# A four-layer gated model on one core: the first cross-attention's keys and values move behind layer 0's first experts, with one unused product, and two row transfers go out a chunk from the eighth chunk

## The chip, the cores and the metric

The kernel runs on one core of one Trainium2 chip. The metric is the device time of one execution, in microseconds (us); several runs are made and their median is compared. The core has five engines with a queue each: TensorE (PE in the profile, with its weight loads as PEld), VectorE (DVE), ScalarE (ACT), GpSimd (POOL) and SyncE (SP, which here only issues transfers). Each works through its own queue in order, and semaphores tie the queues together. All data is float32 but for a mask.

## What is computed

The state X has 16 sequences of 128 tokens with 128 features. It passes four layers. Each layer adds to X a cross-attention with a context C of the same shape, times tanh of a gate, and then a feed-forward part, times tanh of another gate. Cut to what matters here:

```
layer 0: X += g * (Q + tril(C C^T) Q),  Q = norm(X)              # linear attention
         X += g * sum over the best 2 of 8 experts of  c_e * down_e(silu(gate_e x) * up_e x),  x = norm(X)
layer 1: q = norm(X) hW qW,  k = C cW kW,  v = C cW vW           # with biases
         X += g * (softmax(q k^T / sqrt(128)) v + q) oW
         X += g * (best 4 of 16 experts + 2 shared ones)
layers 2 and 3: 16-head attentions, a slot layer, and 32 experts
```

## The kernel before, in words

The 16 sequences are worked in four groups of four (GB = 4), so one tile has 128 features by 512 tokens. Layer 0's experts are done in two ways. Group 0 takes all eight experts densely: 16 chunks of 128 hidden features, each with two products of 128x512 (gate `pg` and up `pu`, in `gated`, L447), an activation on ACT (`sg`), a product `h` on DVE (L464), a product `hw` with the routing weight `cb` (L471 on DVE, L473 on POOL), and a down product into `acc` (L1128), two chunks later. Groups 1 to 3 are routed: their rows are scattered by expert into a table `xd` in HBM by 24 indirect transfers of POOL (`places_0`, L974, tile `xs`), and then worked in blocks of 128 rows that belong to one expert each (`blocks_0`: load `xb` from `xd` on SP's queue at L1040, transposes at L1047, products at L1069, silu at L1076, down product at L1024).

`experts` (L1120) is a generator that writes the whole order of the feed-forward work. While it goes through group 0's chunks n = 0 to 15, it takes steps of other generators in between. `SEND` (L890) says how many of the 24 scatters follow each chunk: 2, 1, 2, 1, 2 for chunks 5 to 9 and 2 for each of 10 to 15, which is 20. Two more follow the last chunk, and the last two are issued only after group 0's next normalisation (`sent_behind` is set to "rs"). A scatter may not pass the latest `hw` product of POOL (`behind_of("hw", ...)`, L112). `on_vector` (L895) says which share of `hw` DVE takes: none for chunks 0 to 4, three quarters for 5 to 9 (POOL takes the last quarter), all from 10. After chunk 9 `joined_1` multiplies the weights of layer 1's attention together in place. After chunk 12 the first half of `attention_1(0)` is taken: keys `kT` (one 128x512 product with L108, copied by ACT with a bias at L288) and values `v` (four 128x128 products, added to a bias by DVE at L591).

When the 16 chunks are done, `acc` is copied to `yT` on ACT (L1131), turned by four transposes (`end`, L1138) and added to X on DVE (L278). Then the second half of `attention_1(0)` runs: statistics on DVE (L251, L255, `ve` at L257), the inverse root `rs` on POOL (L259), the normalised rows `xn` on DVE (L270), four transposes (L241) with a copy to `xnTm` (L243), queries `qT` (L108, L288), scores (L108, `mm<-a,qT`), and the softmax (L313 to L380). The first half of `attention_1(1)` follows in the program, and then the blocks.

Each engine's queue is not the program's order word for word: a list scheduler orders the instructions when the program is built, by their place in the program and by what is ready. `in_turn(chain, ins)` (L439) pins an instruction behind the one before it in a chain, on the order alone. PSUM has four banks for "m" work (attention) and three for "x" work (experts).

Of the kernel before, what the change touches and what calls it, by code (L numbers as in the profile page):

```python
# [10 lines left out]
F32 = mybir.dt.float32  # L11
BF16 = mybir.dt.bfloat16
I32 = mybir.dt.int32
AF = mybir.ActivationFunctionType
ALU = mybir.AluOpType
AX = mybir.AxisListType

P = 128
B = 16
GB = 4  # L20
NG = B // GB
GT = GB * P
D = 128
CH = 512
EPS = 1e-5
# [34 lines left out]
def flamingo(ctx, tc, x_in, ctx_in, mask_in, w1, w2, w3, wslot, wsmall, slots, cols_in, rows_in, consts_in,  # L60
             gu0, dn0, gu1, dn1, gu3, dn3, out):
    nc = tc.nc
# [3 lines left out]
    act = ctx.enter_context(tc.tile_pool(name="act", bufs=2))  # L66
# [21 lines left out]
    def mm_tile():  # L88
        return bank("mm")
# [10 lines left out]
    def bc(ap, axis, n):  # L100

        a = ap.unsqueeze(axis)
        shape = list(a.shape)
        shape[axis] = n
        return a.to_broadcast(shape)

    def mm(o, l, r, start=True, stop=True):
        nc.tensor.matmul(out=o, lhsT=l, rhs=r, start=start, stop=stop)  # L108

    latest = {}  # L110

    def behind_of(what, ins):  # L112

        if what in latest:
            in_turn([latest[what]], ins)
# [65 lines left out]
    ident = const.tile([P, P], F32, tag="ident", name="ident")  # L181
# [32 lines left out]
    for i in range(0, NBLK * D, GB * VB):  # L214
        n = min(GB * VB, NBLK * D - i)
# [3 lines left out]
    def row(name):  # L219
        at, n = ROW[name]  # L220
        return rows[:, at:at + n]

    def col(name):
        i = COLS.index(name)
        return cols[:, i:i + 1]
# [7 lines left out]
    tgf = const.tile([P, 4], F32, tag="tgf", name="tgf")  # L233
    nc.scalar.activation(tgf[:], gates[:, 4:8], AF.Tanh)


    def transposed(src, tag, pool, bufs):

        pt = tr_tile()
        for t in range(GB):  # L240
            nc.tensor.transpose(pt[:, t * P:(t + 1) * P], src[:, t, :], ident[:])  # L241
        o = pool.tile([P, GT], F32, tag=tag, name=tag, bufs=bufs)
        nc.any.tensor_copy(o[:], pt[:])  # L243
        return o

    def normed(g, xn=None, on_act=False, behind=None):
        x = X[g]
        st = small.tile([P, GB, 6], F32, tag=tag_of("st"), name="st")
        mv = small.tile([P, GB, 2], F32, tag=tag_of("mv"), name="mv")
        for t in range(GB):  # L250
            ins = nc.vector.bn_stats(st[:, t, :], x[:, t, :])  # L251
            if t == 0 and behind is not None:
                behind_of(behind, ins)
        for t in range(GB):
            nc.vector.bn_aggr(mv[:, t, :], st[:, t, :])  # L255
        ve = small.tile([P, GB], F32, tag=tag_of("ve"), name="ve")
        nc.vector.tensor_scalar(ve[:], mv[:, :, 1], EPS, None, ALU.add)  # L257
        rs = small.tile([P, GB], F32, tag=tag_of("rs"), name="rs")
        latest["rs"] = nc.gpsimd.tensor_tensor(rs[:], ve[:], neghalf[:], ALU.pow).ins  # L259
        if xn is None:  # L260
            xn = act.tile([P, GB, D], F32, tag=tag_of("xn"), name="xn", bufs=1)
        if on_act:
            off = small.tile([P, GB], F32, tag="off", name="off")
            nc.gpsimd.tensor_tensor(off[:], mv[:, :, 0], rs[:], ALU.mult)
            latest["off"] = nc.gpsimd.tensor_scalar(off[:], off[:], -1.0, None, ALU.mult).ins
        for t in range(GB):
            if on_act:
                nc.scalar.activation(xn[:, t, :], x[:, t, :], AF.Identity, bias=off[:, t:t + 1], scale=rs[:, t:t + 1])
            else:
                nc.vector.tensor_scalar(xn[:, t, :], x[:, t, :], mv[:, t, 0:1], rs[:, t:t + 1], ALU.subtract, ALU.mult)  # L270
        return xn

    def normed_T(g):
        xn = normed(g)
        return xn, transposed(xn, tag_of("xnT"), act, 2 if side[0] == "x" else 1)
# [7 lines left out]
    def linear_T(w, src, tag, bias, bufs=None):  # L283

        p = mm_tile()
        mm(p[:], w, src[:])
        o = act.tile([P, GT], F32, tag=tag, name=tag, bufs=bufs)
        nc.scalar.activation(o[:], p[:], AF.Identity, bias=bias)  # L288
        return o
# [149 lines left out]
    def in_turn(chain, ins):  # L439

        if chain:
            tc.add_manual_dep(ins.ins, chain[-1].name,
                              mybir.DependencyInfo(mybir.DependencyClass.NoSync, mybir.DependencyReason.DATA),
                              reason="in_turn")
        chain[:] = [ins.ins]
# [65 lines left out]
    CT = []  # L511
# [47 lines left out]
    w = lambda W, i: W[:, i * D:(i + 1) * D]  # L559
# [23 lines left out]

    def attention_1(g):

        kT = linear_T(w(W1, 1), CT[g], "a0", bias=col("kb"))
        pv = split(mm_tile())
        for t in range(GB):
            mm(pv[:, t, :], CT[g][:, t * P:(t + 1) * P], w(W1, 2))
        v = act.tile([P, GB, D], F32, tag="a3", name="v1")  # L590
        nc.vector.tensor_tensor(v[:], pv, bc(row("vb"), 1, GB), ALU.add)  # L591
        yield
        _, xnT = normed_T(g)
        (nc.gpsimd if g else nc.vector).tensor_tensor(X[g][:], X[g][:], bc(ob1[:], 1, GB), ALU.add)
        qT = linear_T(w(W1, 0), xnT, "qT", bias=col("qb"))
        ps = split(mm_tile())
        for t in range(GB):
            b = slice(t * P, (t + 1) * P)
            mm(ps[:, t, :], qT[:, b], kT[:, b])
        e = softmax_exp(ps, GB, float(np.float32(1.0) / np.sqrt(np.float32(D))))  # L600
        pn = over_sum(e, P, "sm2", work)
        pts = transpose_probs(pn, P, P)
        po = acc_tile()
        for t in range(GB):
            mm(po[:, t * P:(t + 1) * P], v[:, t, :], pts[:, t, :])
        aT = act.tile([P, GT], F32, tag="oT", name="aT")
        nc.vector.tensor_tensor(aT[:], po[:], qT[:], ALU.add)
        py = split(mm_tile())
        for t in range(GB):
            mm(py[:, t, :], aT[:, t * P:(t + 1) * P], w(W1, 5))  # L610
        add_gated(g, py, tgx[:, 1:2])
        yield
# [274 lines left out]
    routed = {}  # L887


    SEND = [(n, 2 if n > 9 else 1 + n % 2) for n in range(5, 16)]  # L890
    FETCH = {0: [(n, 2) for n in range(4)] + [(n, 1) for n in range(4, 18)], 1: [(n, 1) for n in range(6)]}

    JOIN = 9

    def on_vector(layer, g, n):  # L895

        if (layer, g) == (0, BYE - 1):
            return 1 if n > 9 else 0.75 if n > 4 else 0
        return 1 if (layer, g) == (1, 0) and n < 4 else 0

    def with_tanh(layer, g):
# [218 lines left out]
    def experts():  # L1120


        chain, behind, ends = [], [], []
# [10 lines left out]
        def end():  # L1134
            layer, g, yT = ends.pop()
            pt = split(tr_tile())
            for t in range(GB):
                nc.tensor.transpose(pt[:, t, :], yT[:, t * P:(t + 1) * P], ident[:])  # L1138
            add_gated(g, pt, SHAPE[layer][2])
            if layer == 3:  # L1140
                nc.sync.dma_start(out[g * GB:(g + 1) * GB].rearrange("b s d -> s b d"), X[g][:])
            return layer, g

        for at, (layer, g) in enumerate(ORDER):
# [6 lines left out]
            ne, width, _ = SHAPE[layer]  # L1151
            xnT, cbs = routed.pop((layer, g))
            steps = {}
            moving = (layer, g) == (0, BYE - 1)
            if moving:
                for n, k in SEND:
                    steps.setdefault(n, []).extend([("m", sending, None)] * k)
                steps.setdefault(13, []).append(("m", "owners", None))
                steps.setdefault(JOIN, []).append(("m", joining, None))
                steps.setdefault(JOIN + 3, []).append(("m", context_1, None))  # L1160
            elif at + 1 < len(ORDER):
                nxt = routing(*ORDER[at + 1])
                for n in (12, 14, 15, 17) if (layer, g) == (1, 0) else (3, 7, 8, 13):
                    steps.setdefault(n, []).append(("x", nxt, None))
# [31 lines left out]
                        yield what  # L1196
            if moving:
                side[0] = "m"
                for _ in range(2):
                    next(sending)  # L1200
                side[0] = "x"
                while behind:
                    down()
                what = end()
                side[0] = "m"
                yield what
                sent_behind[0] = "rs"
                for _ in sending:
                    pass
                nxt = routing(1, 0)  # L1210
                for n, _ in enumerate(blocks_0()):
                    if n in (8, 11, 12, 15):
                        side[0] = "x"
                        next(nxt)
                    side[0] = "m"
# [28 lines left out]
    W1 = load("w1", w1)  # L1244
# [9 lines left out]
    sending, fetching = places_0(), return_0()  # L1254
# [10 lines left out]
    context_1 = attention_1(0)  # L1265
# [33 lines left out]
    for s in range(2):  # L1299
        for n in range(2):  # L1300
            nc.vector.tensor_copy(hcols[:, s, 3 * n:3 * n + 1], pp[:, 4 * s + 2 * n:4 * s + 2 * n + 1])
            hcol[f"bq{2 + n}{s}"] = hcols[:, s, 3 * n:3 * n + 1]
            for j in range(2):
                o = hcols[:, s, 3 * n + 1 + j:3 * n + 2 + j]
# [156 lines left out]
```

## Time and profile before

| | |
|---|---|
| median of 3 runs | 897.54 us (896.16 to 898.15) |
| the profiled execution | 894.61 us |
| its span, from first to last instruction | 892.9 us |
| mean granted TensorE clock | 0.979 |
| busy: PE, DVE, POOL, ACT | 92%, 64%, 33%, 30% of the span |
| PE of the chain that ended last | 54% |

The profiled execution is one run with its own time; durations and positions in the text come from it, with the span's start as zero. "Granted clock" is the share of the full TensorE clock that the chip gave: 1.00 or 0.50 nearly everywhere in this trace. A row of the timeline has start, duration, engine, line, operation, what it writes and reads, and in brackets how long the engine stood idle before it and what ended that. A row "x2" or "x8" has several records merged: a float32 product shows as two.

### The profile page before, as it was taken

To read this page: it belongs to the slowest core of one execution; us is meant where nothing else is said; L and a number is where in the kernel's file an instruction comes from. 1 tells how busy PE (TensorE), PEld (TensorE's weight loads), DVE (VectorE), ACT (ScalarE), POOL (GpSimd) and SP (SyncE) were. 2 spreads that over 40 slices of the span, in tenths; PEclk is the share of its full clock that TensorE was granted. 3 is DMA by queue.
4 is the path that set the end of the run, shared out by engine and by line. 5 is a ranking of instruction groups with operands and counts; after the bars stand their busy time and mean duration, and the time that the engine had idled before them with its cause. 6 is when DMAs were issued, how large, how long until landed. Compare 5 with 4: busy or idle time off the path is not lost.

```text
span 892.9 us, 16081 instructions
## 1 busy us (share of the span) xinstructions
PE 825.1 (92%) x6189; PEld 465.7 (52%) x6189; DVE 570.0 (64%) x1599; ACT 263.5 (30%) x473; POOL 296.0 (33%) x304
## 2 busy tenths in 40 slices
PE   6899799988998999998999989999999999999997
PEld 4554599444444544554555554555555544554443
DVE  5775434557878567468667666768766678667522
ACT  1522355232331221332232222232222232222321
POOL 3547321666452123014221114321033122313453
PEclk9999699999999999999999999999999999999999
DMA  9451122840311011002121114110002111111230
GB/s 280 160 124 52 48 83 70 246 127 15 107 60 36 33 41 36 25 25 65 44 61 45 50 37 131 50 37 24 25 25 75 49 37 52 69 49 61 86 113 29
DMA packets 55677, 62.12 MB, mean 70 GB/s; under 512 B 14312, under 2 KB 33512, under 8 KB 55472
## 3 DMA queue, kind: packets, MB, share of 16 engines
q1 hardware_dynamic: 53536, 57.67, 21.1%
q0 software_dynamic: 1536, 3.15, 1.2%
q8 instruction: 49, 0.80, 0.4%
q10 hardware_dynamic: 528, 0.26, 0.1%
q14 instruction: 28, 0.23, 0.1%
HBM read 53.97 MB, written 7.09 MB: 68 GB/s over the span
## 4 chain that ended last, share of the span: by engine, by line
PE 54%; DVE 20%; POOL 10%; issue 9%; ACT 3%; DMA 3%; POOLq 0%; SPq 0%; DVEq 0%; ACTq 0%
PE mm L108 8%; PE pu L453 7%; PE acc L1128 7%; PE pg L452 7%; POOL hw L473 6%; DVE sg L458 3%; PE po L499 3%; DVE mp L493 3%; PE mm L647 3%; DVE h L464 2%; POOL rs L259 2%; PE po L502 2%; PE pg L1069 2%; PE tr L241 2%; DVE xn L270 2%
## 5 line engine op out<-in xcount | busy, mean ns | idle before, releaser
L473 POOL TENSOR_TENSOR hw<-h,cb 128x512 f32<-128x512 f32 (+1 forms) x136 | 171.3, 1260 | 439.5 <-DVE h L464 352.9
L453 PE MATMUL pu<-xnTx,wall 128*128 128x512 f32 x288 | 153.1, 614 | 5.9 <-DVE sg L458 3.7
L452 PE MATMUL pg<-xnTx,wall 128*128 128x512 f32 x288 | 152.8, 613 | 1.1 <-ACT xnTx L243 0.7
L1128 PE MATMUL acc<-hw,wall 128*128 128x512 f32 x288 | 150.1, 605 | 0.5 <-POOL hw L473 0.5
L464 DVE TENSOR_TENSOR h<-sg,pu 128x512 f32<-128x512 f32 x147 | 100.4, 683 | 69.2 <-PE pu L453 57.7
L457 ACT ACTIVATE sg<-pg 128x512 f32<-128x512 f32 x105 | 62.8, 598 | 222.0 <-PE pg L452 213.4
L458 DVE SCALAR_TENSOR_TENSOR sg<-sg,pg 128x512 f32<-128x512 f32 x105 | 71.3, 679 | 32.9 <-ACT sg L457 32.8
L453 PEld LDWEIGHTS pu<-xnTx,wall 128*128 128x128 f32 x288 | 51.7, 192 | 65.7 <-issue 42.3
L1128 PEld LDWEIGHTS acc<-hw,wall 128*128 128x128 f32 x288 | 53.2, 194 | 56.0 <-issue 48.6
L493 DVE TENSOR_REDUCE mp<-mm 128x4 f32<-128x512 f32 (+1 forms) x112 | 65.7, 644 | 21.1 <-PE mm L647 19.9
L452 PEld LDWEIGHTS pg<-xnTx,wall 128*128 128x128 f32 x288 | 49.5, 192 | 40.5 <-issue 29.5
L507 DVE RECIPROCAL rcw<-po 128x128 f32<-128x128 f32 (+1 forms) x28 | 25.2, 900 | 52.8 <-PE po L502 41.9
L460 ACT ACTIVATE sg<-pg 128x512 f32<-128x512 f32 x51 | 30.4, 596 | 81.9 <-PE pg L452 81.8
L259 POOL TENSOR_TENSOR rs<-ve,neghalf 128x4 f32<-128x4 f32 x32 | 32.8, 1026 | 61.4 <-DVE ve L257 60.0
L499 PE MATMUL po<-pts,vp 128*32 128x128 f32 (+1 forms) x896 | 45.8, 273 | 6.4 <-ACT pts L669 5.5
L270 DVE TENSOR_SCALAR xn<-x,mv,rs 128x128 f32<-128x128 f32 x104 | 36.7, 408 | 21.5 <-POOL rs L259 21.5
L669 ACT ACTIVATE pts<-mm 128x512 f32<-128x512 f32 x64 | 33.8, 600 | 54.8 <-PE mm L663 54.3
L502 PE MATMUL po<-pts,own 128*32 128x128 f32 (+1 forms) x896 | 43.9, 265 | 0.0
L499 PEld LDWEIGHTS po<-pts,vp 128*32 128x32 f32 (+1 forms) x896 | 21.5, 108 | 29.4 <-ACT pts L669 14.3
L251 DVE BATCH_NORM_STATS2 st<-x 128x6 f32<-128x128 f32 x128 | 30.8, 301 | 8.9 <-DMA x<-in_x 8.3
L241 PE MATMUL tr<-ident,xn 128*128 128x128 f32 x100 | 23.3, 316 | 12.7 <-DVE xn L270 11.5
L647 PE MATMUL mm<-kTm,qT 32*128 32x256 f32 x256 | 30.5, 413 | 0.0
(354 smaller groups left out, 1234.4 us busy)
## 6 DMA issues: line engine op xcount, KB each, us to landing
cb<-combD SPq DMA_DIRECT2D x72, 256.0 KB, 3.4
cb<-combD SPq DMA_DIRECT2D x128, 128.0 KB, 2.9
wall<-in_gu SPq DMA_DIRECT2D x24, 256.0 KB, 5.0
wall<-in_dn SPq DMA_DIRECT2D x12, 256.0 KB, 4.8
xb<-xd SPq DMA_DIRECT2D x7, 256.0 KB, 2.8
yd<-yb SPq DMA_DIRECT2D x7, 256.0 KB, 2.3
xd<-vp SPq DMA_DIRECT2D x1, 1072.0 KB, 7.5
x<-in_x SPq DMA_DIRECT2D x4, 256.0 KB, 6.5
```

What stands on the lines that cost most here:

```text
L108: nc.tensor.matmul(out=o, lhsT=l, rhs=r, start=start, stop=stop)
L452: in_turn(chain, nc.tensor.matmul(out=pg[:], lhsT=w[:, 0], rhs=xnT[:], start=True, stop=True))
L453: in_turn(chain, nc.tensor.matmul(out=pu[:], lhsT=w[:, 1], rhs=xnT[:], start=True, stop=True))
L457: nc.scalar.activation(sg[:], pg[:], AF.Tanh, scale=0.5)
L458: nc.vector.scalar_tensor_tensor(sg[:], sg[:], 1.0, pg[:], ALU.add, ALU.mult)
L464: ins = nc.vector.tensor_tensor(h[:], sg[:], pu[:], ALU.mult)
L473: latest["hw"] = nc.gpsimd.tensor_tensor(hw[:, at:], h[:, at:], cb[:, at:], ALU.mult).ins
L493: nc.vector.tensor_reduce(mp[:, 0:n, 32 * i + 16:32 * i + 18], src, AX.X, ALU.max)
L499: in_turn(chain, nc.tensor.matmul(out=po[32 * jj:32 * jj + 32, 0, :], lhsT=vcols, rhs=pts, start=first, stop=last, skip_group_check=True))
L502: in_turn(chain, nc.tensor.matmul(out=po[32 * jj:32 * jj + 32, 1, :], lhsT=own[rows, r, :], rhs=pts, start=False, stop=last, skip_group_ch ...
L647: nc.tensor.matmul(out=split(ps[i])[:, 2 * s:2 * s + 2, :], lhsT=qT[rr, s, b], rhs=kTm[rr, s, :, b], start=False, stop=True, skip_group_ch ...
L1128: in_turn(chain, nc.tensor.matmul(out=acc[0][:], lhsT=w[:, 2], rhs=h[:], start=n == 0, stop=last))
```

## The change

Four edits:

1. The first half of `attention_1(0)` is no longer taken after chunk 12. The generator now runs through in one go, when group 0's experts are done. For group 0 the products are pinned on PE in this order: the four transposes of `yT`, keys, values, an unused product, the four transposes of `xn`. The normalisation stands ahead of the keys in the program, and DVE's addition for `v` is pinned behind `ve`.
2. `busy_with(512)` is the unused product: the identity by four copies of itself, into a bank of PSUM that nobody reads.
3. `SEND` gives two scatters to chunk 8 as well, so 21 fall to the chunks, one follows the last chunk instead of two, and the last two stay behind the normalisation.
4. `on_vector` gives all of `hw` to DVE from chunk 8 instead of chunk 10.

For the other groups `attention_1` does what it did.

```diff
+    def busy_with(n, chain=None):
+        o = mm_tile()[:, :n].rearrange("p (t d) -> p t d", d=P)
+        ins = nc.tensor.matmul(out=o, lhsT=ident[:], rhs=bc(ident[:], 1, n // P), start=True, stop=True)
+        if chain is not None:
+            in_turn(chain, ins)
...
-        nc.vector.tensor_scalar(ve[:], mv[:, :, 1], EPS, None, ALU.add)
+        latest["ve"] = nc.vector.tensor_scalar(ve[:], mv[:, :, 1], EPS, None, ALU.add).ins
...
     def attention_1(g):
-        kT = linear_T(w(W1, 1), CT[g], "a0", bias=col("kb"))
+        chain = [latest["yT"]] if g == 0 else None
+        if g == 0:
+            xn = normed(g)
+        p = mm_tile()
+        mm(p[:], w(W1, 1), CT[g][:], chain=chain)
+        kT = act.tile([P, GT], F32, tag="a0", name="a0")
+        nc.scalar.activation(kT[:], p[:], AF.Identity, bias=col("kb"))
         pv = split(mm_tile())
         for t in range(GB):
-            mm(pv[:, t, :], CT[g][:, t * P:(t + 1) * P], w(W1, 2))
+            mm(pv[:, t, :], CT[g][:, t * P:(t + 1) * P], w(W1, 2), chain=chain)
         v = act.tile([P, GB, D], F32, tag="a3", name="v1")
-        nc.vector.tensor_tensor(v[:], pv, bc(row("vb"), 1, GB), ALU.add)
-        yield
-        _, xnT = normed_T(g)
+        ins = nc.vector.tensor_tensor(v[:], pv, bc(row("vb"), 1, GB), ALU.add)
+        if g == 0:
+            behind_of("ve", ins)
+            busy_with(CH, chain)
+            xnT = transposed(xn, "xnTm", act, 1, chain)
+        else:
+            yield
+            _, xnT = normed_T(g)
...
-    SEND = [(n, 2 if n > 9 else 1 + n % 2) for n in range(5, 16)]
+    SEND = [(n, 2 if n > 7 else 1 + n % 2) for n in range(5, 16)]
...
         if (layer, g) == (0, BYE - 1):
-            return 1 if n > 9 else 0.75 if n > 4 else 0
+            return 1 if n > 7 else 0.75 if n > 4 else 0
...
-                nc.tensor.transpose(pt[:, t, :], yT[:, t * P:(t + 1) * P], ident[:])
+                latest["yT"] = nc.tensor.transpose(pt[:, t, :], yT[:, t * P:(t + 1) * P], ident[:]).ins
...
-                steps.setdefault(JOIN + 3, []).append(("m", context_1, None))
...
             if moving:
                 side[0] = "m"
-                for _ in range(2):
-                    next(sending)
+                next(sending)
```

More of the change, by code (lines that the diff above doesn't have):

```diff
@@ L105, in bc, with mm @@
         return a.to_broadcast(shape)
-    def mm(o, l, r, start=True, stop=True):
-        nc.tensor.matmul(out=o, lhsT=l, rhs=r, start=start, stop=stop)
+    def mm(o, l, r, start=True, stop=True, chain=None):
+        ins = nc.tensor.matmul(out=o, lhsT=l, rhs=r, start=start, stop=stop)
+        if chain is not None:
+            in_turn(chain, ins)
     latest = {}
@@ L234, in flamingo, with transposed @@
     nc.scalar.activation(tgf[:], gates[:, 4:8], AF.Tanh)
-    def transposed(src, tag, pool, bufs):
+    def busy_with(n, chain=None):
+        o = mm_tile()[:, :n].rearrange("p (t d) -> p t d", d=P)
+        ins = nc.tensor.matmul(out=o, lhsT=ident[:], rhs=bc(ident[:], 1, n // P), start=True, stop=True)
+        if chain is not None:
+            in_turn(chain, ins)
+    def transposed(src, tag, pool, bufs, chain=None):
         pt = tr_tile()
         for t in range(GB):
-            nc.tensor.transpose(pt[:, t * P:(t + 1) * P], src[:, t, :], ident[:])
+            ins = nc.tensor.transpose(pt[:, t * P:(t + 1) * P], src[:, t, :], ident[:])
+            if chain is not None:
+                in_turn(chain, ins)
         o = pool.tile([P, GT], F32, tag=tag, name=tag, bufs=bufs)
```

## The prediction, made before the changed kernel ran

> **What bounds the kernel now.** I read the page's slices first. PE is 90% busy nearly everywhere, and the row of its granted clock has one dip, in slice 5 (89 to 112 us), just where the change works.
>
> ```profile
> PEclk9999699999999999999999999999999999999999
> ```
>
> The busy table by stretches then shows the dip's edges. I cut it at 3.41 us, since the clock changes only at multiples of that (91.48, 108.54, 183.63, 217.76).
>
> ```profile
> core 0: us, PE busy (x) PEld busy (x) DVE busy (x) ACT busy (x) POOL busy (x), PEclk, DMA share, GB/s
> 88.07:91.48 3.41, 1.54 (x6) 0.47 (x5) 1.12 (x3) 0.59 (x1) 2.79 (x4) 1.00 0.12 38
> 91.48:94.89 3.41, 0.77 (x3) 0.55 (x3) 2.21 (x12) 0.00 (x0) 2.42 (x3) 0.50 0.06 19
> 101.72:105.13 3.41, 2.73 (x13) 2.55 (x13) 1.38 (x3) 2.88 (x4) 0.00 (x0) 0.50 0.05 15
> 105.13:108.54 3.41, 3.41 (x18) 3.41 (x18) 1.62 (x4) 1.86 (x3) 0.61 (x1) 0.50 0.00 0
> 169.98:173.39 3.41, 1.78 (x5) 0.60 (x4) 1.35 (x5) 0.60 (x1) 2.92 (x4) 1.00 0.91 301
> 214.35:217.76 3.41, 1.55 (x10) 1.08 (x10) 1.92 (x12) 0.61 (x1) 2.23 (x3) 1.00 0.08 19
> 217.76:221.17 3.41, 3.41 (x7) 1.46 (x6) 3.11 (x13) 0.60 (x1) 1.75 (x3) 0.50 0.02 5
> ```
>
> A stretch with 1.54 or 1.55 of 3.41 us busy (45%) was followed by half clock; one with 1.78 (52%) was not. A cold stretch with 2.73 (80%) stayed cold; one that was full brought the clock back. So PE is cold from 91.48 to 108.5.
>
> The timeline of all engines between the experts and the blocks, and the waits of SP's queue, tell what the stage waits for.
>
> ```profile
> 91.14 0.62 POOL L1063 COPY wb<-wall 128x512 f32 x1
> 92.29 0.17 DVE L257 TENSOR_SCALAR ve<-mv 128x4 f32<-128x4 f32 x1
> 92.55 1.04 POOL L259 TENSOR_TENSOR rs<-ve,neghalf 128x4 f32<-128x4 f32 x1 [0.79 <-DVE ve L257]
> 95.20 1.28 POOL L974 DMA_INDIRECT xd<-xs,to  x1 [0.30 <-issue]
> 97.89 13.52 SPq L1040 DMA_DIRECT2D xb<-xd  x4
> 98.98 2.08 PE L108 MATMUL mm<-a,qT 128*128 128x128 f32 x8 [0.78 <-ACT qT L288]
> 100.85 1.06 PE L1047 MATMUL tr<-ident,xb 128*128 128x128 f32 x4
> 102.59 2.08 PE L1069 MATMUL pg<-xbT,wb 128*128 128x128 f32 x8 [0.68 <-ACT xbT L1049]
> ```
>
> ```profile
> SPq L1040 <- DMA xd<-xs,to: 30.3, 1, 30.3
> ```
>
> Two chains run from `rs` and end together at 101 us. One is the attention on the cold PE, whose scores end at 101.06. The other is POOL's last scatter: it ends at 96.48, SP's load of the first rows waited for it until 97.89, and the rows land about 3 us later (median to landing 2.9), when their transposes start (100.85). From 102.59 PE has no gap for 50 us, so the end moves with the blocks.
>
> **Keys and values leave the chunks.** These are the two rows on PE's timeline:
>
> ```profile
> 77.47 1.02 PE L108 MATMUL mm<-cT,w 128*128 128x512 f32 x2
> 78.33 1.05 PE L108 MATMUL mm<-w,cT 128*128 128x128 f32 x8
> ```
>
> By the starts (77.47, 78.33, next 79.22) they take 0.86 + 0.89 = 1.75 us. PE is full from 67 to 88, so all that follows comes 1.75 us earlier: `yT`'s transposes end at 88.54 instead of 90.29, `ve` at 90.71 instead of 92.46.
>
> In the gap the same 1.75 us stand again, plus the unused product, which has the keys' shape: 0.86. Sum 2.61, from 88.54 to 91.15. The gap is 94.12 - 90.29 = 3.83 us, so PE is done 1.2 us ahead of the next transposes; cost nothing. If the clock were half already there, it would be up to 5.2 us, 1.4 too much; but the stretch before it is busy, so I exclude that. ACT's 0.69 us for the keys falls in its idle 5.9 us. DVE's addition for `v` (0.69) now stands between `ve` and `xn`, and waits for the values (90.29). It runs from about 90.8 to 91.5, and `xn` behind it waits for `rs` until 92.1 in any case: nothing, with 0.6 us of cover. If the values came later than that, `xn` and all behind it would slip one for one.
>
> **POOL.** The scatters are a queue of 22 ahead of `rs` both before and after (20 + 2, 21 + 1). What changes is that two quarter products `hw` go:
>
> ```profile
> 66.86 0.96 POOL L974 DMA_INDIRECT xd<-xs,to  x1 [0.30 <-issue]
> 67.85 0.47 POOL L473 TENSOR_TENSOR hw<-h,cb 128x128 f32<-128x128 f32 x1
> 68.48 1.01 POOL L974 DMA_INDIRECT xd<-xs,to  x1 [0.16 <-issue]
> ```
>
> With `hw`, the next scatter starts 0.66 us after the last one's end (67.82 to 68.48); without, it is the usual 0.30. Two such places give 2 x 0.36 = 0.72 us, not twice 0.6. So POOL's 22nd scatter ends at 90.4 instead of 91.13, the copy `wb` behind it at 91.04 instead of 91.76, and `rs` starts at 91.1: POOL has become 0.35 us later than `ve` (90.71). Bounds: 90.8, if the scheduler puts `wb` elsewhere (-1.75), and 92.2, if POOL wins nothing there and an extra copy falls ahead of `rs` (-0.3). I take -1.45, since `wb` sits there now. DVE takes 2 x (0.69 - 0.56) = 0.26 us more for the whole `hw`; the down products come two chunks (5 us) later, so nothing waits.
>
> **What is late next.** Everything behind `rs` keeps its distances: two scatters, 1.41 us to SP's release, 3 us to land. The rows' transposes start at 100.85 - 1.45 = 99.4. On a warm PE the attention would be far ahead: transposes 92.7 to 93.3 (0.66, as at 89.63), copy, queries 0.86, copy 0.69, scores 0.89, end at 96.6. So PE then idles 2.8 us for the rows: the attention's warm clock is worth nothing to the end by itself.
>
> **Does the clock hold?** The Trainium skill (TensorE: Matmul & The Clock Gate, "Why this matters for your kernels") says to leave no gap over about 3 us between matmuls, since one idle window halves the clock. After the change the longest gaps are 1.2, 0.7 and 2.8 us, so by the rule the clock stays up, and the sum is that of the first rival, -4.2. The rows say otherwise: at 217.76 the clock halved though the longest gap in the stretch before was 1.77 us; the stretch was only 45% busy. From 91.15 to 100.5 PE has 0.66 + 0.86 + 0.89 + 0.5 = 2.9 us of work in 9.3, some 30%, and a whole stretch lies inside wherever the grid falls. I go by the rows: cold again before the block products. The rows' transposes then take between 0.49 and 1.06 us; halfway is -0.3 (bounds -0.57, 0).
>
> The clock returned 5.92 us after the first block product (102.59 to 108.51). A full stretch is needed, so the wait is 3.4 to 6.8, by where the grid falls; the middle, 5.1, saves half of 0.8 us, and some of the cold time may fall ahead of the blocks: -0.5 (bounds -1.25, +0.45).
>
> **Sum.** -1.45 - 0.3 - 0.5 = -2.25 us. Against the profiled execution's own 894.61 that is 892.4; the runs' median is 2.9 us higher, and the same difference gives 897.54 - 2.25 = 895.3. This case's own range is 893.9 to 897.0 (-3.6 to -0.5, by the bounds).
>
> **Rivals.**
>
> *The clock stays up* (15%). For it: the unused product, and the skill's rule. Against: the 45% rows. Transposes warm -0.57; then from the first block product to the end of the second `pu` it was 6.94 us (102.59 to 109.53). Warm, ACT's chain rules: load 1.28, exp 0.63, load 1.28, silu 0.60 = 3.8 us until a bank is free, then 0.9: 4.75, so -2.19. Sum -1.45 - 0.57 - 2.19 = -4.2: 893.3.
>
> *The gain doesn't arrive* (15%). POOL holds `rs` at its bound of -0.3 because the scatters don't come closer together or another copy is queued there. The chunks end sooner and wait. 897.2.
>
> *The clock returns two stretches later* (20%), slower. The blocks' first products now meet rows that come early while ACT still loads its tables for exp and silu, so PE has pockets. From 0.7 us of idle in a stretch on (the 80% row) that stretch does not bring the clock back; each costs 1.71 us. For it: four block products and ACT's 3.8 us stand side by side. Against: the cold PE had no gap there before. -1.45 + 2 x 1.71 = +2.0: 899.5.
>
> **How the numbers follow.** A measurement of this kernel tells about 0.2%, 1.8 us, from no change. Of the likeliest case's 50 chances in a hundred, 33 lie below -1.8 us and 17 between that and no change. Faster: 33 + 15 = 48. Same: 17 + 15 = 32. Slower: 20. The range runs from 892.8, a little under the warm case, to 899.0, short of the slow one; it leaves out some 5 chances below and 14 above.
>
> **What would show it.** Keys and values at 88.5 to 90.3 with PE full up to there; `rs` at about 91.1 behind POOL, not `ve`; SP's load released at 96.4; idle PE before the rows' transposes at 99.4; half clock at the first block product. Wrong if the scheduler orders ACT so that exp passes the copy of the rows, which would draw softmax work into the idle 2.8 us, or if it lets `rs` pass the scatters, or if later stages are reordered.

## The result, and the profile after

The changed kernel took 902.38 us (median of 7 runs, 900.28 to 904.53), the kernel before, beside it, 897.37 us (7 runs, 895.87 to 898.15): ratio 1.0069, 95% interval 1.0054 to 1.0085. It is 5.0 us slower by the medians. (Ratios and intervals here and below are those on record, estimated over all runs; they need not be the quotient of the two medians.) Forecast were 895.3 us and a range of 892.8 to 899.0.

The profiled execution took 902.38 us, its span 900.7. The rows of PE's busy tenths and of its granted clock, in 40 slices:

```profile
PE   5897699979988999998999999999999999999997
PEclk9899899999999999999999999999999999999999
```

Slices 4 and 5, counted from 1 (67 to 112 us), have 7 and 6 tenths of work on PE, where the page of before has 9 and 7. The clock in slice 5 is 0.8 instead of 0.6: its dip is less deep, but PE stands still for longer.

In the kernel before, ACT answers a gate product of these chunks at once. The product ends at 80.24, its silu `sg` starts at 80.34:

```profile
79.22 1.02 PE L452 MATMUL pg<-xnTx,wall 128*128 128x512 f32 x2
...
80.34 0.60 ACT L460 ACTIVATE sg<-pg 128x512 f32<-128x512 f32 x1 [1.12 <-PE pg L452]
```

The timeline of all engines after the change, from the last chunks to the first block product:

```profile
77.11 1.02 PE L463 MATMUL pg<-xnTx,wall 128*128 128x512 f32 x2
...
84.43 0.60 ACT L471 ACTIVATE sg<-pg 128x512 f32<-128x512 f32 x1 [6.51 <-remote]
85.08 2.08 PE L464 MATMUL pu<-xnTx,wall 128*128 128x512 f32 x2 [4.27 <-issue]
...
102.72 0.17 DVE L268 TENSOR_SCALAR ve<-mv 128x4 f32<-128x4 f32 x1
...
102.98 1.04 POOL L270 TENSOR_TENSOR rs<-ve,neghalf 128x4 f32<-128x4 f32 x1 [5.88 <-DVE ve L268]
...
111.16 0.66 PE L1070 MATMUL tr<-ident,xb 128*128 128x128 f32 x4 [1.68 <-DMA xb<-xd]
...
112.49 2.08 PE L1092 MATMUL pg<-xbT,wb 128*128 128x128 f32 x8 [0.68 <-ACT xbT L1072]
```

Up to 77 us PE runs as forecast: keys and values are gone, it is full. Then a gate product ends at 78.13, and ACT, which waits for nothing else, starts its `sg` at 84.43: the signal took 6.3 us. PE, without `sg` and with its banks full, stops for 4.27 us (and again for 0.70 and 2.32), is at half clock from 84.95 to 88.36 and from 91.78 to 98.61, and the transposes of `yT` come at 100.06, not at 88. From there on the steps come in the order forecast, with PE's wait for the rows (1.68 us, not 2.8) and half clock at the first block product; but `rs` waits for `ve` (5.88 us), not for POOL.

The trace also lists the updates of the semaphores. From 60 to 100 us it has 303 of them after the change and 722 before; of the 16 updates with which each scatter reports, 0 to 5 are listed where one lands between 70 and 90 us. Over the whole run there are 8,428 against 9,123. So in this execution signals came late, and many left no record. I call this **late signals**.

The listed updates tell whose signals they were. From 60 to 106 us the listed updates of ACT, DVE and POOL each stand within 0.06 us of the end of one of the engine's instructions. Of PE's 33, nine do not. Taken in order, the gate product that ended at 78.13 is reported at 84.35, and the up product behind it (end 79.10) at 88.55; five more reports then come from 92.05 to 92.22, about 0.04 us apart. POOL's stream of scatters had moved its last packet at 89.83. So of the engines' signals PE's alone were late here, and the burst says that they had queued until the stream was over. Whether the scatters' own reports were late cannot be told, since most left no record.

It is not the change alone that makes them. The runs were made in groups, each with the kernel before in it. The median of the kernel before was 892.2 to 892.7 us in four groups and 895.9 to 897.4 in three (the recorded result among these), with the same program. The 12 traces of the first kind, over all kernels, list 9,115 to 9,124 updates, and in none of them does an update of PE come late between 60 and 106 us; the eight of the second list 8,221 to 8,491, with 6 to 13 late updates of PE. One chip gave both kinds in different groups. The trace that the forecast was made from lists 9,123: it is of the first kind, though the median of the runs given beside it was of the second. So each experiment is read beside the kernel before of its own group. I call the kinds **quick** and **late**. What decides between them is open. Every time on record comes with a span and a clock from a trace, so it is untested, too, whether taking the trace has a part in it.

### The profile page after: what moved, and what is told of

Same layout as the page of the kernel before. It is cut to its first block, busy times and chain, and to the rows that moved or that the text cites. A ratio compares the mean times of both kernels' runs of the same rounds, so it can differ in the third digit from the quotient of the medians.

```text
span 900.7 us, 16080 instructions
## 1 busy us (share of the span) xinstructions
PE 825.2 (92%) x6191; PEld 463.4 (51%) x6191; DVE 572.3 (64%) x1599; ACT 263.4 (29%) x473; POOL 292.9 (33%) x302
## 4 chain that ended last, share of the span: by engine, by line
PE 53%; DVE 20%; POOL 10%; issue 10%; DMA 3%; ACT 3%; SPq 0%; POOLq 0%; another core or an unknown queue 0%; DVEq 0%; ACTq 0%
PE pu L464 7%; PE mm L108 7%; PE acc L1151 7%; PE pg L463 6%; POOL hw L484 6%; PE po L510 3%; DVE sg L469 3%; DVE mp L504 3%; DVE h L475 2%; PE mm L670 2%; POOL rs L270 2%; PE po L513 2%; PE pg L1092 2%; PE mm L686 2%; PE tr L250 2%
## 5 line engine op out<-in xcount | busy, mean ns | idle before, releaser
L1151 PE MATMUL acc<-hw,wall 128*128 128x512 f32 x288 | 152.8, 615 | 0.5 <-POOL hw L484 0.5
```

What stands on the lines that cost most here:

```text
L1151: in_turn(chain, nc.tensor.matmul(out=acc[0][:], lhsT=w[:, 2], rhs=h[:], start=n == 0, stop=last))
```

## The experiments

Places are compared in microseconds after the first `counts` product of the routing on PE (49 to 53 us into a span), since it does not come at the same time in each span. "Turned" is the start of the transposes, "blocks done" the start of the transposes of `comb`, which come just before the last down product of the blocks. Each row is one profiled execution:

| kernel | kind | `yT` turned | rows turned | first block product | blocks done | end |
|---|---|---|---|---|---|---|
| before, as predicted from | quick | 39.10 | 50.32 | 52.06 | 104.69 | 842.34 |
| before again (e7) | quick | 39.09 | 50.30 | 52.04 | 102.72 | 840.34 |
| change (e5) | quick | 37.34 | 48.55 | 50.34 | 102.36 | 839.82 |
| change without the product (e6) | quick | 37.34 | 48.55 | 50.29 | 102.70 | 839.84 |
| all sent, no product (e8) | quick | 36.40 | 42.01 | 43.79 | 99.22 | 837.35 |
| all sent (e9) | quick | 36.41 | 42.23 | 43.89 | 97.33 | 833.29 |
| before (e13) | late | 41.33 | 53.38 | 55.17 | 106.87 | 843.82 |
| change, recorded | late | 49.90 | 60.99 | 62.32 | 113.65 | 850.50 |
| change (e10) | late | 50.09 | 61.20 | 62.53 | 113.86 | 853.62 |
| move alone (e14) | late | 38.97 | 53.07 | 54.81 | 106.31 | 842.84 |
| transfers alone (e15) | late | 53.04 | 64.26 | 66.00 | 117.47 | 854.33 |
| loads later (e16) | late | 48.11 | 59.15 | 60.94 | 113.52 | 850.91 |

### First group (quick): the parts

**e1_move**: edits 1 and 2 alone, that is the change with the kernel before's `SEND` and `on_vector` (`n > 9`).

> Edits 1 and 2 alone (keys and values moved, unused product), transfers and hw as before. Theory T, the transfers: in the changed kernel the scatters run back to back from 66 us and the semaphore updates of PE, ACT and DVE come late between 75 and 92 us; that is the doing of edits 3 and 4. Then this kernel has no late updates, the chunks end 1.75 us earlier, rs waits for POOL (91.8 instead of 92.55), and the time is 0.5 to 2.5 us under before. Rival M, the move: the late updates come with the products taken out of the chunks. Then this kernel shows them too (ACT's sg of the last chunks late by 6 us) and is 3 to 7 us over before.

Measured 892.45 us against 892.61, ratio 1.0007 (0.9989 to 1.0026).

**e2_transfers**: edits 3 and 4 alone, in the kernel before:

```diff
-    SEND = [(n, 2 if n > 9 else 1 + n % 2) for n in range(5, 16)]
+    SEND = [(n, 2 if n > 7 else 1 + n % 2) for n in range(5, 16)]
...
-            return 1 if n > 9 else 0.75 if n > 4 else 0
+            return 1 if n > 7 else 0.75 if n > 4 else 0
...
-                for _ in range(2):
-                    next(sending)
+                next(sending)
```

> Edits 3 and 4 alone (two scatters from chunk 8, all of hw on DVE from chunk 8), keys and values where they were. Theory T: the late updates are here, the last chunks stall, 3 to 8 us over before. Rival M: no late updates; rs is bound by ve as before, so the time is within 0.5 us of before.

892.30 against 892.61, 1.0001 (0.9990 to 1.0013).

**e3_no_product**: the change without `busy_with(CH, chain)`.

> The changed kernel without the unused product. By both theories the stall in the last chunks has nothing to do with it: 3 to 7 us over before, within 1.5 us of the changed kernel. If the clock in the gap matters, PE is cold at the queries and scores (1.9 us instead of 0.9 each), and the time grows by at most 2 us over the changed kernel, since the rows' transposes wait for the load.

891.11 against 892.61, 0.9984 (0.9971 to 0.9996).

**e4_vector**: edit 4 alone, the second line pair of e2's diff.

> Edit 4 alone: DVE takes all of hw from chunk 8, the scatters' number for each chunk as before. POOL's scatters close up by 2 x 0.36 us as in the changed kernel. If it is closing up that brings the late updates (theory T), they are here too, with 3 to 8 us over before; if it takes the one more scatter in chunk 8, or the move (rival M), the time is within 0.5 us of before.

892.64 against 892.61, 1.0002 (0.9991 to 1.0014).

No part stopped PE, and none cost anything. Either the parts had to come together, or the measurement was of another kind.

### Second group (quick): the whole change

**e5_after_again**: the change, unaltered.

> The changed kernel once more, beside the kernel before on the same chip, since none of its parts alone was slower by more than 0.2% and none showed late semaphore updates. If the late updates belong to the combination of all four edits (theory C), they are here again: ACT's sg of the last chunks 6 us late, 3 to 7 us over before. If they were a condition of the earlier chip or program load and not of the edits (rival L), this kernel shows no late updates, its chunks end 1.75 us earlier, the rows' transposes start about 1.5 us earlier than before, and the time lies 0 to 2 us under before.

891.92 against 892.51 (22 runs), 0.9993 (0.9983 to 1.0003). My theory that only the combination stalls fell: nothing stalled, with the same program and the same order on every engine as in the recorded result.

**e6_no_product_again**: e3's kernel, beside it.

> The changed kernel without the unused product, on the same chip as the run of the whole change. Theory C (the product is needed for the stall): 0.5 to 2 us under before, and the whole change 3 to 7 us over it. Rival L: this and the whole change agree within 1 us, both 0 to 2 us under before.

891.05, 0.9983 (0.9973 to 0.9992). Without the product the median is 0.9 us lower than e5's; the intervals overlap, and the two traces end together (839.82 and 839.84), so what the product costs stays open.

PE's timeline of e5 shows the forecast's stage, undisturbed:

```profile
88.83 1.02 PE L241 MATMUL mm<-ident 128*128 128x512 f32 x2
...
94.83 1.16 PE L108 MATMUL mm<-a,qT 128*128 128x128 f32 x8 [0.78 <-ACT qT L299]
97.79 1.11 PE L1070 MATMUL tr<-ident,xb 128*128 128x128 f32 x4 [1.80 <-DMA xb<-xd]
99.58 2.08 PE L1092 MATMUL pg<-xbT,wb 128*128 128x128 f32 x8 [0.68 <-ACT xbT L1072]
101.45 1.92 PE L1092 MATMUL pu<-xbT,wb 128*128 128x128 f32 x8
103.15 1.59 PE L1092 MATMUL pg<-xbT,wb 128*128 128x128 f32 x8
```

The attention runs warm (scores 1.16 us), PE waits 1.80 us for the rows, and then is cold at the first three block products. The kernel before in e7's trace has it the other way round:

```profile
97.99 2.08 PE L108 MATMUL mm<-a,qT 128*128 128x128 f32 x8 [0.78 <-ACT qT L288]
99.86 1.06 PE L1047 MATMUL tr<-ident,xb 128*128 128x128 f32 x4
101.59 1.16 PE L1069 MATMUL pg<-xbT,wb 128*128 128x128 f32 x8 [0.68 <-ACT xbT L1049]
```

It is cold while PE waits anyway, and warm from the first block product on. So the change starts the blocks 1.70 us earlier (50.34 for 52.04) and ends them 0.36 us earlier (102.36 for 102.72): 1.34 us are lost on the way, where the clock is the difference that the rows show.

### Third group (quick): send the rows earlier

**e7_before_again**: the kernel before, for its trace.

> The kernel before, once more, for its trace on the chip of the other runs and as a test of the comparison. Its ratio to itself is 1.000 within 0.15%. Theory G (the gain arrives in the stage and stays): its trace is later than the changed kernel's by 2 to 3 us at the products of the second group's keys, and by the same at the end. Rival P (the gain is taken back later): later by 2 to 3 us there, and by less than 1 us at the end of the blocks or after the wait for layer 1's weights at 171 us.

892.53 against 892.16, 1.0002 (0.9992 to 1.0013).

**e8_all_sent_no_product** and **e9_all_sent**: the change, without and with the product, and with all 24 scatters issued by the end of the last chunk:

```diff
-    SEND = [(n, 2 if n > 7 else 1 + n % 2) for n in range(5, 16)]
+    SEND = [(n, 2) for n in range(5, 16)]
...
-            return 1 if n > 7 else 0.75 if n > 4 else 0
+            return 1 if n > 4 else 0
...
-                next(sending)
+                for _ in range(2):
+                    next(sending, None)
```

> The changed kernel without the unused product, with two scatters after every chunk from 5 and all of hw on DVE from chunk 5, so that all 24 scatters end before ve. If the rows' load (the last scatter, 1.4 us to SP, 3 us to land) bounds the blocks' start in the changed kernel, the rows now land about 5 us earlier, the rows' transposes follow the scores without a wait, the blocks start 2 to 3 us earlier, and the time is 2 to 4 us under before if the gain of the stage stays. If the rows' load is not the bound, within 0.5 us of the kernel without the product (891.1).

889.44 against 892.16, 0.9965 (0.9951 to 0.9978).

> The same with the unused product. Now no wait for rows follows the scores, so a clock kept up in the gap can last: PE is at full clock at the first block product, and this one is 0.5 to 2.5 us under the one without the product. If the product doesn't hold the clock (less than half of a 3.41 us stretch busy), the two agree within 0.7 us.

885.91, 0.9931 (0.9912 to 0.9949): 6.3 us faster than the kernel before, and faster than both. The rows are turned 8 us earlier (42.23 for 50.30; PE still waits 2.56 us for them), the first block product comes before the attention's transposes are done, and PE hardly waits after it:

```profile
93.47 0.99 PE L1070 MATMUL tr<-ident,xb 128*128 128x128 f32 x4 [2.56 <-DMA xb<-xd]
94.25 0.85 PE L250 MATMUL tr<-ident,xn 128*128 128x128 f32 x3
95.14 0.80 PE L1092 MATMUL pg<-xbT,wb 128*128 128x128 f32 x2
```

Here the product is worth 3.5 us by the medians. One reason shows in the traces: e9 is cold for one stretch of 3.41 us from there, e8 for two.

### Fourth group (late): the stall is back

**e10_after_third**: the change, unaltered.

> The whole change once more, unaltered. If the late signals of the recorded result belong to the conditions of that measurement and not to the edits, the ratio is again 0.998 to 1.000, PE shows no stop between 75 and 95 us, and the rows' transposes come 1.7 to 1.8 us earlier than in the kernel before, counted from the routing's counts. If the change itself provokes the late signals on some chips, a ratio near 1.005 to 1.007 with a stop of 4 to 6 us on PE may come back here.

904.48 against 895.89, 1.0072 (1.0047 to 1.0097), 8,425 updates listed. The recorded result repeats, stop included (3.73 us on PE, before the `pu` behind this `sg`):

```profile
80.71 1.12 PE L463 MATMUL pg<-xnTx,wall 128*128 128x512 f32 x2 [0.24 <-DVE h L475]
...
84.92 0.60 ACT L471 ACTIVATE sg<-pg 128x512 f32<-128x512 f32 x1 [6.49 <-remote]
```

**e11_sent_alone**: e8's three edits of the transfers in the kernel before, nothing moved.

> All 24 transfers out by the time of ve, but keys and values left in the chunks and no product. If the rows' load alone bounds the stage, most of the gain of the run with everything (0.9931, with the product; 0.9965 without) comes without the move: about 0.996 to 0.997, with the rows' transposes some 8 us earlier than before. If the move is what lets the attention stand beside the blocks, it stays at 0.999 to 1.001. The clock: without the 2.6 us of work in the hole PE is some 40% busy over a 3.41-us stretch, so half clock for some stretches again, which would leave 2 us of the 6 behind.

897.35, 1.0021 (1.0010 to 1.0033), with stops of 1.6, 3.7 and 3.6 us on PE from 72 to 91 us. Its rows were turned 0.50 us after `yT`'s transposes, so the wait for the rows is gone; the late signals take more than that brings. It met the late kind alone, so what sending all rows brings without the move where signals are quick is not measured.

**e12_after_filled**: the change, with two more unused products where PE waits for the rows:

```diff
-            mm(ps[:, t, :], qT[:, b], kT[:, b])
+            mm(ps[:, t, :], qT[:, b], kT[:, b], chain=chain)
+        if g == 0:
+            for _ in range(2):
+                busy_with(CH, chain)
```

> The whole change, and two more unused products (0.86 us each) behind the first attention's scores, where PE idled 1.80 us for the rows. If the clock is where the predicted gain went (the first three block products took 2.08, 1.92 and 1.59 us instead of 1.06 to 1.16), PE stays warm there and the blocks start 2.3 us faster: about 889.6 against 891.9 without, ratio 0.9965 to 0.998. If ACT's table loads and copies bound the blocks' start anyway, PE just waits instead: 0.999 to 1.000. If the products fall later than the idle, up to 1.7 us slower, 1.001.

904.43, 1.0076 (1.0050 to 1.0102): as slow as e10, since the late signals stand ahead of it. The forecast of the total missed; the part that it was made for did what was expected. The two products, and the first block product, which is now warm:

```profile
106.74 2.50 PE L241 MATMUL mm<-ident 128*128 128x512 f32 x4
...
110.45 1.16 PE L1095 MATMUL pg<-xbT,wb 128*128 128x128 f32 x8 [0.78 <-DVE xbT L1075]
```

From the first block product to the end of the blocks it took 50.07 us; e10, with one cold stretch there, 51.33; e5, with most of two, 52.02. PE's order inside differs a little, so not all of the difference need be the clock.

### Fifth group (late): which half

**e13_before_slow**: the kernel before, one run, for its trace.

> The kernel before, for its trace beside the others of this call. If the measurement is of the kind in which the kernel before takes 895 to 897 us, its trace shows late signals too, a stop on PE of 1 to 4 us between 70 and 90 us; if the late signals come with the change alone, none. If this measurement is of the 892-us kind, no stop anywhere.

896.79 us; 8,436 updates. It has late signals too, but only at the end of the chunks: the first late update of PE stands at 84.67 us, and `yT` is turned 2.2 us later than in e7.

**e14_move_again**: e1's kernel.

> The move and the product alone; the transfers as in the kernel before. If the transfers sent earlier are what brings the 5 to 7 us where signals come late, this stays within 0.3% of the kernel before also where that takes 896 us: 0.998 to 1.001. If the move is, 1.006 to 1.007. In the 892-us kind both give 1.000.

895.01 against 897.34, 0.9978 (0.9962 to 0.9994). Late signals cost it no more than they cost the kernel before. ACT's copy of `yT` and the transposes behind it:

```profile
87.56 0.58 ACT L1154 COPY yT<-acc 128x512 f32<-128x512 f32 x1 [4.52 <-remote]
...
88.20 0.66 PE L1161 MATMUL tr<-ident,yT 128*128 128x128 f32 x4 [2.29 <-issue]
```

The last down product ended at 85.9, so this signal took 1.7 us.

**e15_transfers_again**: e2's kernel.

> The transfers alone, keys and values left in the chunks. If the transfers bring the late signals, 1.006 to 1.008 where the kernel before takes 896 us, with PE's stop at 77 to 90 us; if the move or its product does, 0.999 to 1.001. In the 892-us kind 1.000.

906.93, 1.0094 (1.0062 to 1.0125; 5 runs). The transfers' half brings the stall by itself, worse than the whole change. All engines in it:

```profile
78.04 1.02 PE L108 MATMUL mm<-cT,w 128*128 128x512 f32 x2
...
90.48 0.69 ACT L288 ACTIVATE a<-mm,cols 128x512 f32<-128x512 f32 x1 [9.23 <-remote]
93.33 0.69 DVE L591 TENSOR_TENSOR v<-mm,rows 128x512 f32<-128x512 f32 x1 [8.38 <-remote]
...
94.08 2.07 PE L453 MATMUL pu<-xnTx,wall 128*128 128x512 f32 x2 [8.68 <-ACT sg L460]
```

The keys' product ends at 79.06, and ACT learns of it at 90.48, 11.4 us later (PE's update is listed at 90.46). The silu of the next gate product stands behind it on ACT's queue, and PE behind that.

**e16_loads_later**: the change, with the 16 loads of weights by head, which SP issues from 55 to 66 us, moved behind the blocks' last rows:

```diff
-                    behind_of("spread", nc.sync.dma_start(o[:, :, DK * j:DK * j + DK], a[:, j]))
+                    behind_of("xb", nc.sync.dma_start(o[:, :, DK * j:DK * j + DK], a[:, j]))
...
-                nc.sync.dma_start(xb[:, 0:q, :], rows_of(xd, b0, q))
+                latest["xb"] = nc.sync.dma_start(xb[:, 0:q, :], rows_of(xd, b0, q)).ins
```

> The whole change, with the 16 loads of the weights by head, 8192 pieces of 32 bytes issued between 55 and 66 us, moved on SP's queue behind the blocks' last rows (about 135 us). The traces with late signals begin to miss signals in just that stretch. If this burst is what the signals hang behind, no stop on PE is left, and the ratio falls from 1.007 to about 1.000 where the kernel before takes 896 us; in the 892-us kind it stays at 0.999. The moved loads may hold the second experts' weights on SP's queue by up to 5 us, of which 1 to 4 us may reach the end (up to 1.004). If the burst is not the cause, the stop at 77 to 90 us stands as before.

902.98, 1.0064 (1.0047 to 1.0081). The stop stands as it was, so that burst is not the cause:

```profile
82.37 1.12 PE L463 MATMUL pg<-xnTx,wall 128*128 128x512 f32 x2 [0.24 <-DVE h L475]
87.21 1.12 PE L464 MATMUL pu<-xnTx,wall 128*128 128x512 f32 x2 [3.72 <-ACT sg L471]
```

### Sixth group (quick): which of the two edits

**e17_quarters_back**: the change, with `on_vector` as before (`n > 9`): edit 4 undone.

> The change, but chunks 8 and 9 leave a quarter of hw with POOL as before; two transfers a chunk from the eighth stay. POOL's stream of transfers then has its two short pauses back (0.66 instead of 0.30 us between two transfers, twice). If it is the unbroken stream that brings the late signals, PE does not stop between 75 and 90 us, and where the kernel before takes about 896 us the ratio is 0.997 to 0.999, as for the move alone (0.9978); if the number of transfers out by then is what counts, 1.006 to 1.007. Where the kernel before takes 892 us, 0.998 to 1.001 by both.

891.41 against 892.65, 0.9988 (0.9977 to 0.9999).

**e18_vector_moved**: the change, with `SEND` (and two after the last chunk) as before: edit 3 undone.

> The change, but the transfers are asked for as in the kernel before (two a chunk from the tenth only); chunks 8 and 9 do all of hw on DVE as in the change. With no hw between them the transfers stand in POOL's queue one behind the other all the same, in the order of the whole change. If the unbroken stream brings the late signals: 1.006 to 1.008 where the kernel before takes about 896 us, with PE's stop. If sending earlier does it, not the missing pauses: 0.997 to 0.999. Where the kernel before takes 892 us, 0.999 to 1.000.

892.35, 0.9993 (0.9981 to 1.0004), e5's ratio to the digit.

This group was of the quick kind, so neither run can say which edit brings the late signals. One thing they settle without times: on every engine's queue the instructions stand in e18 in the order of the whole change. A scatter may not pass POOL's last `hw`; once chunks 8 and 9 leave POOL no `hw`, nothing holds the scatters apart, whatever `SEND` says. Edit 3 therefore adds nothing of its own to edit 4.

## Why the prediction failed

**The step that failed** is "PE is full from 67 to 88, so all that follows comes 1.75 us earlier", together with the price of "POOL", where two quarter products less were counted as 0.72 us won and nothing else. In the recorded measurement PE was not full: it stopped for 4.27, 0.70 and 2.32 us between 80 and 93 us and was cold for 10.24 us between 84 and 99 us, and `yT` was turned at 49.90 after the counts instead of 37.34. Beside the late trace of the kernel before (e13), the blocks are done 6.8 us later and the span ends 6.7 us later, so the whole loss arises here. The edit that I priced as a gain is the one that costs: the transfers alone give 1.0094 in the late kind, the move alone 0.9978. None of my rivals had it. They all lay behind the chunks; the price lay inside them, on queues that the edit doesn't touch.

What is shown: the late signals belong to the kind of measurement (the kernel before has them, with a tail of 2 us), of the engines' signals they are PE's alone, and the transfers' half makes them come some 8 to 10 us earlier, inside the chunks, where PE needs ACT's answer within 2 us (in e5 `sg` ends at 77.89 and the next `pu` stands at 79.61). The half's mark on POOL is that its stream of scatters has no `hw` in it from 65 or 66 us on (change, e15), and only from 69 or 71 us on in e14 and e13. The first signals that stop PE came at 78 (change), 81 (e15), 86 (e14) and 89 us (e13). By the listed updates PE's lateness begins at 71 to 77 us in the six late traces in which DVE takes all of `hw` from chunk 8 or 5, and at 85 and 86 us in e13 and e14. In seven of the eight it ends in a burst of waiting signals, 1.5 to 2.5 us after the stream's last packet; in e13 a last single one comes 1.1 us after it. That fits a backlog of PE's signals that fills while the scatters run close together and empties when they end.

What is not shown is whether the scatters themselves hold PE's signals up, by which path, and why in some measurements only: e9, in the quick kind, sent its scatters without `hw` between them from 62.5 us on and has no late update. That it is the missing pauses is argued as well: e17, which puts them back, met the quick kind. The small loads are excluded by e16.

Two steps of the forecast's sum were unsound beside this, though neither makes the miss. It put a difference worked out from a quick trace onto the median of late runs (897.54). And its bounds add up to -3.57 and +0.15 us, not to "-3.6 to -0.5".

**Where signals were quick**, the forecast's steps can be checked one by one (e5 against e7):

- *Keys and values.* Forecast -1.75; `yT` is turned 1.75 us earlier (37.34 for 39.09). Right.
- *POOL.* Forecast -1.45 for `rs`, bounds -1.75 and -0.3. Counted from the counts it came 1.75 us earlier, behind `ve` and not POOL. The 22nd scatter ended 1.75 us earlier (38.85 for 40.60 in the trace predicted from), not 0.72, so the copy `wb` ended in time. Besides the two quarter products, single scatters got shorter: the 9th took 1.27 us and takes 0.96, the 16th 1.39 and 0.96. The forecast did not have this; why they do is not shown.
- *The hole.* 2.61 us of work forecast at no cost. Right: the transposes of `xn` waited for `xn` for 1.13 us all the same.
- *The rows.* Forecast that PE then waits 2.8 us for them; 1.80. Their transposes on a warm PE were to bring -0.3; from their start to the first block product it took 1.79 us, where e7 took 1.74: nothing.
- *Clock lost.* Right, and by the mechanism named. The table by stretches of e5:

```profile
core 0: us, PE busy (x) PEld busy (x) DVE busy (x) ACT busy (x) POOL busy (x), PEclk, DMA share, GB/s
90.62:94.03 3.41, 2.27 (x6) 0.85 (x6) 1.95 (x5) 0.58 (x1) 2.38 (x2) 1.00 0.08 26
94.03:97.45 3.42, 1.19 (x9) 0.97 (x8) 1.38 (x2) 0.69 (x1) 0.00 (x0) 1.00 0.44 127
97.45:100.86 3.41, 2.40 (x10) 2.00 (x11) 0.00 (x0) 1.89 (x3) 0.00 (x0) 0.50 0.40 116
100.86:104.27 3.41, 3.41 (x18) 3.41 (x18) 2.17 (x4) 2.48 (x3) 0.61 (x1) 0.50 0.03 5
```

  A stretch with 1.19 of 3.42 us busy (35%) halves the clock though its longest gap is 1.80 us; one with 2.27 (67%) does not. The Trainium skill's gap of about 3 us (TensorE: Matmul & The Clock Gate, "Why this matters for your kernels") would have kept it up; the measurement decides for the share.
- *Clock's price.* Forecast -0.5, bounds -1.25 and +0.45; it was +1.34 (1.70 us at the first block product, 0.36 at the blocks' end). I took the cold time of the kernel before from one execution, and that was the longest of three: 17.07 us in the trace predicted from, 10.24 in e7, 13.65 in e13. In e7 the clock came back after this stretch,

```profile
97.98:101.39 3.41, 2.93 (x12) 2.52 (x12) 1.25 (x2) 0.44 (x1) 0.00 (x0) 0.50 0.80 230
```

  with 2.93 of 3.41 us busy (86%), so a full stretch, as I had it, isn't needed. Against the trace predicted from, e5's blocks end 2.33 us earlier (102.36 for 104.69), almost the forecast's 2.25; against e7's, 0.36.
- *Sum.* -2.25 forecast; -0.6 us measured (0.9993, 0.9983 to 1.0003), no change that can be told. The rest is mainly the clock's term. With late signals the move alone, without the transfers, gained 2.3 us by the medians.

## What to carry to other kernels

An edit to a stream of transfers is priced on the whole core, not on its own queue: ask which engine needs another's signal within two microseconds while the stream runs, and take a second measurement at another time before believing either sign. A phase of the clock read from one execution is one draw; look at what the kernel before does in a second trace before counting on cold time to be saved. Bringing forward what really ends the stage (the rows, by sending all transfers early, on top of the change) made the kernel 6.3 us faster than before in the quick kind, where shifting work ahead of it was worth 0.6; but that kernel was never measured in the late kind, where sending them all, alone, lost (1.0021).

## What the runs showed of the hardware

The kernel before had two kinds of measurement: medians of 892.2 to 892.7 us, with 9,123 and 9,124 semaphore updates in its traces, and of 895.9 to 897.4 us, with 8,436 (e13). In the second kind ACT could start 6.3 us (change) or 11.4 us (e15) after the end of the PE product that it waited for, where 0.10 us is seen in the quick trace of before; the profile calls such a wait "remote" or "issue". From 60 to 106 us only PE's updates were late, 6 to 13 in a trace, and they came out in a burst 1.5 to 2.5 us after the last packet of POOL's scatters in seven traces of eight. The clock came back after a stretch that was 86% busy, where the trace predicted from had shown 80% not to be enough.
